# First quartic of the late images: a transpose on TensorE replaced by a block transpose on VectorE and four DMAs

## The chip, the cores and the metric

The kernel runs on one core of a Trainium2 chip. The metric is the device time of one execution in microseconds (us). Several executions of the kernel before gave 2962.28, 2969.88 and 2977.81 us, median 2969.88.

Names in the profile: PE is TensorE (PEld its weight loads), DVE is VectorE, ACT is ScalarE, POOL is GpSimd, SP is SyncE, which here only issues DMAs. SPq and ACTq are the DMA issues on those two engines.

## The reference, cut to what matters

```python
# x: 32 images, 32 channels, 128 x 128, float32
def layer0(A):                       # per image and channel: five steps of Newton-Schulz
    Y = A / norm(A); Z = I
    for _ in range(5):
        T = 0.5 * (3 * I - Z @ Y)
        Y = Y @ T
        Z = T @ Z
    return Y * sqrt(norm(A))
x = x + layer0(groupnorm(x))
def layer1(x):                       # 2-D Fourier transform, 64 x 32 modes, a channel product, back
    s = real(fft2(x))
    top = einsum('bixy,ioxy->boxy', s[:, :, :32, :32], weights1)
    bot = einsum('bixy,ioxy->boxy', s[:, :, -32:, :32], weights2)
    return real(ifft2(top and bot in a zero array))
x = x + layer1(groupnorm(x))
```

So each of the 1024 matrices of 128 x 128 goes through a polynomial in itself, and each image then through a transform, a product over channels and a transform back. The kernel merges the five steps into two quartics in the matrix, with the updates of `y` and `m` between them, and a last product.

## The kernel before

**Tiles and lanes.** A tile is four channels of one image, [128, 4, 128] floats, 256 KB; an image has 8 tiles, all images 256. One tile's Newton iteration is a Python generator, `newton` (line 479), with a `yield` between its steps. Up to 9 such generators are "lanes". The main loop (line 1132) runs in rounds; in each round every lane takes one step. `rest` is two yields. Whatever a step issues goes to the engines in that order, and an outer layer (`InOrder`, line 73) keeps the order of the program on every engine. Line 88 is the helper through which every instruction is recorded, so the profile shows L88 almost everywhere and groups are told apart by tile names.

**Far and near.** Images 1 to 18 are "far" (`is_far`, line 357): their transposed matrices are made by a 32 x 32 block transpose on DVE (`turned`, line 421) and DMAs that move the blocks (`across`, four DMAs of 64 KB from tile to tile; `away` and `back`, by way of DRAM). A new far tile starts every 26/9 rounds. Image 0 and images 19 to 31 are "near": transposes are done by TensorE (`transposed`, line 351), 4 per block. A new near tile starts every 5 rounds (`NEAR`), at most 5 lanes of them at a time (`LESS`); a near tile takes rounds 0 to 23 of its lane. There are 104 tiles in images 19 to 31.

**A near tile, by rounds of its lane.** `near_quartic` (line 407): in round 0 TensorE forms `products(mb, m)` (4 matmuls), DVE adds to make `v`; in round 1 POOL makes `r = mb + eye`; in round 2 TensorE transposes `v` and DVE makes `w` from that and `r`; in round 4 TensorE forms `products(v, w)` and DVE makes `q`; two rounds later it returns. Then `y` (round 6), the new matrix `m` (round 8), its transpose `mb` (TensorE and ACT, round 10), the second `near_quartic` (rounds 12 to 18), a pair of products of 256 columns (round 18), `t` (20) and the last product with DVE's addition to `xt` (22).

**Around the lanes.** `staged` (line 375) normalizes the next tile while a tile starts: `m` from `xt` (the transposed input) and `mb` from `b`. In near tiles POOL makes the four channels of `m` and ACT those of `mb`; in far tiles ACT makes two of the four of `m` as well. `fetch` (line 366) issues the two loads two tiles ahead, on SP for far images, on ACT for near ones. `prep` (line 222) loads an image pair's statistics input `xs` on the ACT queue, three loads ahead, one step per round while the first memory pools live. `settle` (line 538) stores a finished tile to `mid` on SP, and POOL folds it. Spectra and channel products follow per group of images (`GROUPS`, 20, 7, 3 and 2 images); `inverse` (line 970) runs beside the late lanes in three of ten rounds: it loads `yt` (512 KB each) on SP, TensorE transforms back, ACT copies `d`, DVE adds, POOL subtracts and adds `d` into `yt` (`unfold`), and `store` (line 932) writes `out` on SP at the next step of `inverse`. Images 0 to 19 are transformed back at about 1850 to 2390 us of the profile, the seven after them at about 2550 to 2750 us.

**Memory.** `rooms` (line 308) gives for each kind of tile how many buffers rotate in the pool that lives to the end and in the pool that is given up when the group of 20 images is nearly done (from tile 158 on only the first number counts). PSUM is 8 banks that rotate. A write into a rotated buffer waits until the last reader is done. A DMA is issued by its engine in order: where it must wait for data or a buffer, everything behind it on that engine waits too.

Of the kernel before, what the change touches and what calls it, by code (L numbers as in the profile page):

```python
# [31 lines left out]
ALU = mybir.AluOpType  # L32
# [16 lines left out]
MS = 1 / QR  # L49
# [44 lines left out]
def conv_preact_kernel(  # L94
# [49 lines left out]
        od.append(dram.tile(shape, F32, name=f"od{i}", tag=f"od{i}"))  # L144
    where = [(i, b) for i, n in enumerate(GROUPS) for b in range(n)]

    stp = ctx.enter_context(tc.tile_pool(name="stp", bufs=4))
    up = ctx.enter_context(tc.tile_pool(name="up", bufs=1))
    sp = ctx.enter_context(tc.tile_pool(name="sp", bufs=1))
    small = ctx.enter_context(tc.tile_pool(name="small", bufs=1))  # L150
# [71 lines left out]
    def prep(bs, made):  # L222

        n = len(bs)
        nc_, ng = n * C, n * G
        first_b = bs[0]
        st = small.tile([P, ng, 6], F32, tag="a_st", name=f"a_st{first_b}", bufs=2)
        tiles = []
        parts = [(b, i) for b in bs for i in range(C // 4)]

        ahead = 3 if first_b else 8

        def load(k):
            b, i = parts[k]
            if first_b or i < 4:
                t = stp.tile([P, 2, 2 * P], F32, tag="xs", name=f"xs{b}_{i}")
            else:
                t = four("turn", True).rearrange("p (j c) x -> p j (c x)", j=2)
            src = xs_in[b, :, 2 * i : 2 * i + 2].rearrange("p g h c -> p g (h c)")
            kept(nc.scalar.dma_start(out=t, in_=src))  # L240
            tiles.append(t)

        for k in range(ahead):
            load(k)
        yield
        for k in range(len(parts)):
            for j in range(2):
                nc.vector.bn_stats(st[:, 2 * k + j, :], tiles[k][:, j, :])
            yield
            if k + ahead < len(parts):  # L250
                load(k + ahead)
        ms = small.tile([P, ng], F32, tag="a_ms", name=f"a_ms{first_b}")
        nm, d = yield from moments(st, ms, "a")
        yield from pause
        pq = bank()[:, 0, 0:nc_]
        nc.tensor.matmul(pq, avg_mean, d.rearrange("p g c -> p (g c)"), start=True, stop=True)
        if not first_b:
            warm(5)

        v = small.tile([P, nc_ + ng], F32, tag="a_v", name=f"a_v{first_b}")  # L260
        nc.vector.tensor_scalar_mul(v[:, 0:nc_], pq, -512 / (P * P))
        yield
        vg = small.tile([P, ng], F32, tag="a_vg", name=f"a_vg{first_b}")
        nc.vector.tensor_reduce(
            vg, v[:, 0:nc_].rearrange("p (g c) -> p g c", c=2), AX.X, ALU.add
        )
        nc.vector.tensor_scalar(v[:, nc_:], vg, 0.5, EPS, ALU.mult, ALU.add)
        yield
        s = small.tile([P, nc_ + ng], F32, tag="a_r_s", name=f"a_r_s{first_b}", bufs=2)
        yield from root(v, nc_ + ng, s)  # L270
        iv = small.tile([P, nc_ + ng], F32, tag="a_inv", name=f"a_inv{first_b}")
        nc.vector.reciprocal(iv, s)
        yield

        sc = small.tile([P, nc_], F32, tag="a_sc", name=f"a_sc{first_b}", bufs=2)
        nc.vector.tensor_scalar_mul(sc, iv[:, 0:nc_], MS / P)
        off = small.tile([P, ng, 2], F32, tag="a_off", name=f"a_off{first_b}", bufs=2)
        nc.vector.tensor_tensor(
            off,
            sc.rearrange("p (g c) -> p g c", c=2),  # L280
            nm[:, :, None].to_broadcast([P, ng, 2]),
            ALU.mult,
        )
        off = off.rearrange("p g c -> p (g c)")
        sn = small.tile([P, nc_], F32, tag="a_t_s", name=f"a_t_s{first_b}", bufs=3)
        for k, b in enumerate(bs):
            g, c = slice(k * G, k * G + G), slice(k * C, k * C + C)
            made[b] = (nm[:, g], sc[:, c], off[:, c], sn[:, c])
        yield
        nn = small.tile([P, ng, 2], F32, tag="a_d", name=f"a_n{first_b}")  # L290
        nc.vector.tensor_tensor(
            nn,
            s[:, 0:nc_].rearrange("p (g c) -> p g c", c=2),
            iv[:, nc_:, None].to_broadcast([P, ng, 2]),
            ALU.mult,
        )
        nn = nn.rearrange("p g c -> p (g c)")
        for far in sorted({is_far(b) for b in bs}):
            of = [k for k, b in enumerate(bs) if is_far(b) == far]
            c = slice(of[0] * C, of[-1] * C + C)  # L300
            f = EYE_Q * QS if far else EYE * QF
            nc.vector.tensor_scalar_mul(nn[:, c], nn[:, c], P * (1.5 / f) ** 2)
        yield
        yield from root(nn, nc_, sn)
        yield


    rooms = dict(b=(4, 6), xt=(10, 5), x=(3, 2), r=(4, 0), v=(3, 2), w=(3, 2), q=(4, 2))
    rooms.update(my=(4, 3), mb=(2, 4), t=(3, 2), y4=(2, 2), turn=(0, 4))
    turns = dict.fromkeys(rooms, 0)  # L310

    def four(tag, more):
# [44 lines left out]
    def is_far(b):  # L357
        return 0 < b < FIRST
# [5 lines left out]
    raw = {}  # L364

    def fetch(b, g):
        queue = nc.sync if is_far(b) else nc.scalar
        xt, t = four("xt", has_more(b, g)), four("b", has_more(b, g))
        kept(queue.dma_start(out=t, in_=x[b, :, 4 * g : 4 * g + 4, :]))
        kept(queue.dma_start(out=xt, in_=xt_in[b, :, 4 * g : 4 * g + 4, :]))  # L370
        raw[b, g] = xt, t
# [3 lines left out]
    def staged(b, g, nm, sc, off, sn):  # L375
# [9 lines left out]

        for j in range(4):
            c = 4 * g + j
            if j < 2 or not is_far(b):
                kept(
                    nc.gpsimd.tensor_scalar(  # L390
                        m[:, j, :],
                        xt[:, j, :],
                        nm[:, c // 2 : c // 2 + 1],
                        sc[:, c : c + 1],
                        ALU.add,
                        ALU.mult,
                    )
                )
            else:
                on_scalar(m[:, j, :], xt[:, j, :], off, sc, c)  # L400
            on_scalar(mb[:, j, :], mb[:, j, :], off, sc, c)
            yield
# [4 lines left out]
    def near_quartic(m, mb, more):  # L407


        v = plus(m, -QA * MS, products(mb, m), "v", more)  # L410
        yield
        r = four("r", more)
        nc.gpsimd.tensor_tensor(r, mb, eye, ALU.add)
        yield
        w = plus(transposed(v), 1.0, r, "w", more)
        yield from rest
# [19 lines left out]
        kept(nc.sync.dma_start(out=into, in_=src))  # L436
        return t

    def by_rows(t):
        return blocks(t).rearrange("p a c j -> p c a j")  # L440

    def across(t, more):

        w = four("w", more)
# [7 lines left out]
            )  # L452
        return w

    def far_quartic(m, mb, v, f, later, more):

        ps = products(m, mb)
        if later:
            held = away(turned(ps, more))
        else:  # L460
            w = across(turned(ps, more), more)
        if later:
            yield
        nc.vector.scalar_tensor_tensor(v, ps, 1 / (9 * MS), v, ALU.mult, ALU.add)
        if not later:
            yield
# [9 lines left out]

    rest = (None, None)

    def newton(g, sn, xt, m, mb, v, far, more):


        qf, et, eye_t = (QS, EYE_Q, eye_q) if far else (QF, EYE, eye)
        if far:
            q = yield from far_quartic(m, mb, v, 1.0, False, more)
        else:
            q = yield from near_quartic(m, mb, more)
        my = four("my", more)
# [23 lines left out]
        else:  # L511
# [2 lines left out]
            mb = taken(transposed(m), "mb", more)  # L514
            yield from rest
            q = yield from near_quartic(m, mb, more)
            both = [bank().rearrange("p (j k) x -> p j k x", k=2) for _ in range(2)]
            for j in range(4):
                nc.tensor.matmul(both[j // 2][:, j % 2], q[:, j], my[:, j], start=True, stop=True)
# [223 lines left out]
    def small_products(i):  # L743
# [37 lines left out]
            load_weights(kk)  # L781
        for k2 in range(len(xks)):
            load_spectra(k2)
        done = None
        for kk in range(KK):
            yield
# [78 lines left out]
    def weights():  # L865


        kinds = [("b", 2)] * 3 + [("x", 2), ("b", 4), ("x", 4), ("x", 10)]
        kinds += [("my", 11)] * 2 + [("r", 12)] * 3 + [("mb", 15)] * 2 + [("v", 15)] * 2
        kinds += [("w", 16)] * 2 + [("my", 16), ("r", 17), ("v", 18)] + [("q", 19)] * 3  # L870
        first = B * C // 4 - 10
        spare = []
        for half in range(4, 2 * KK):
# [56 lines left out]
    stores = []  # L930

    def store():
        while stores:
            b, o, y = stores.pop(0)
            kept((nc.scalar if tail else nc.sync).dma_start(out=out[b, :, o : o + 8, :], in_=y))

    sums = []
# [2 lines left out]
    def unfold():  # L940

        while sums:
            b, o, y, d = sums.pop(0)
            engine = nc.vector if tail and o % 16 else nc.gpsimd
            for half, op in enumerate((ALU.subtract, ALU.add)):
                yh = y[:, :, 64 * half : 64 * half + 64]
                engine.tensor_tensor(yh, yh, d, op)
            stores.append((b, o, y))

    placed = {}  # L950

# [180 lines left out]
    while todo or any(lanes) or posts or specs or prods or backs:  # L1132
# [3 lines left out]
        for i in range(LANES):  # L1136
# [1 line left out]
            step(loads)  # L1138
            far = todo and is_far(todo[0][0])
            under_way = [is_far(lane[0]) for lane in lanes if lane]  # L1140
            room = far or under_way.count(False) + 0.6 * under_way.count(True) < LESS
            if lanes[i] is None and todo and room and rounds >= due:
                due = max(due, rounds - 1) + (FAR if far else NEAR)
                while norms:
                    step(norms)
                b, g = todo.pop(0)
                xt = ready[0][0]
                lanes[i] = (b, g, xt, newton(g, made[b][3], *ready.pop(0), far, has_more(b, g)))
                if stages:
                    stage()  # L1150
                if not todo:
# [11 lines left out]
                step(specs)  # L1163
            if i == 3 or tail:
                step(posts)
            turn = rounds % 10 in (0, 3, 7)
            if i == 0 and not turn or tail:
                step(prods)
# [72 lines left out]
```

## Time and profile before

| what | value |
|---|---|
| median of the runs | 2969.88 us |
| the profiled execution's own time | 2972.83 us |
| its span, first to last instruction | 2971.0 us |
| around the span | 1.8 us |
| granted clock of TensorE, mean | 0.987 |
| busy PE, DVE, POOL, ACT | 2847.8, 2270.9, 1986.9, 1544.7 us |
| HBM read and written | 402.42 MB, 229.11 MB |
| DMA, mean | 227 GB/s |

The busy shares are shares of the span. A group's line gives the count, the busy time in all, the mean duration of one in ns, and the idle time of its engine just before, with what ended that idle time. Matmuls overlap: the mean duration of one is longer than the distance from one to the next. A float32 matmul of 128 columns is two instructions in the profile, a transpose is one, so a block of four matmuls shows as x8 and a block of four transposes as x4. The span falls into: image 0 and the start (to about 60 us), the far images (to about 1500 us), near images alone or with the wide channel products (to about 1850 us), near images beside the way back of 20 images (to about 2390 us), channel products and the way back of seven (to about 2750 us), and the end.

### The profile page before, as it was taken

To read this page: it belongs to the slowest core of one execution; us is meant where nothing else is said; L and a number is where in the kernel's file an instruction comes from. 1 tells how busy PE (TensorE), PEld (TensorE's weight loads), DVE (VectorE), ACT (ScalarE), POOL (GpSimd) and SP (SyncE) were. 2 spreads that over 40 slices of the span, in tenths; PEclk is the share of its full clock that TensorE was granted. 3 is DMA by queue.
4 is the path that set the end of the run, shared out by engine and by line. 5 is a ranking of instruction groups with operands and counts; after the bars stand their busy time and mean duration, and the time that the engine had idled before them with its cause. 6 is when DMAs were issued, how large, how long until landed. Compare 5 with 4: busy or idle time off the path is not lost.

```text
span 2971.0 us, 74313 instructions
## 1 busy us (share of the span) xinstructions
PE 2847.8 (96%) x27688; PEld 2666.9 (90%) x27688; DVE 2270.9 (76%) x4407; ACT 1544.7 (52%) x3899; POOL 1986.9 (67%) x2308
## 2 busy tenths in 40 slices
PE   7999999999999999999999999999999999999995
PEld 7899999998999999999999889888888999888983
DVE  7779788888788888888886645886787766777565
ACT  3555555555555555555544445555555544655552
POOL 4677777776767777777665534877778764678453
PEclk9999999999999999999999999999999999999997
DMA  5687878787787878787843566767767747766577
GB/s 174 185 250 244 242 242 251 240 257 231 233 252 217 275 228 263 236 253 239 270 145 98 164 209 210 269 217 271 269 228 268 273 127 222 218 223 225 180 221 260
DMA packets 553078, 674.22 MB, mean 227 GB/s; under 512 B 99344, under 2 KB 333840, under 8 KB 552720
## 3 DMA queue, kind: packets, MB, share of 16 engines
q1 hardware_dynamic: 480576, 536.53, 56.9%
q10 hardware_dynamic: 72144, 132.94, 14.3%
q8 instruction: 222, 3.64, 0.5%
q14 instruction: 136, 1.11, 0.1%
HBM read 402.42 MB, written 229.11 MB: 213 GB/s over the span
## 4 chain that ended last, share of the span: by engine, by line
PE 66%; POOL 11%; DMA 9%; issue 7%; DVE 5%; ACT 1%; SPq 1%; ACTq 0%; DVEq 0%; POOLq 0%
PE ps L88 66%; POOL yt L88 3%; POOL r L88 3%; POOL x L88 2%; DMA w<-turn 2%; POOL fold L88 2%; DMA yt<-mid 1%; DMA b<-in_x 1%; DMA xt<-in_xt 1%; SPq L88 1%; DVE turn L88 1%; DMA xs<-in_xs 1%; DVE yt L88 1%; DMA mid<-xt 1%; DMA out<-yt 1%
## 5 line engine op out<-in xcount | busy, mean ns | idle before, releaser
L88 ACT ACTIVATE my<-ps 128x512 f32<-128x512 f32 x512 | 305.3, 600 | 563.6 <-PE ps L88 443.7
L88 POOL TENSOR_TENSOR fold<-xt 128x256 f32<-128x256 f32 x512 | 363.5, 732 | 285.9 <-DVE xt L88 257.2
L88 ACT ACTIVATE b<-b,a_off,a_sc 128x128 f32<-128x128 f32 x1024 | 469.8, 493 | 97.1 <-issue 15.9
L88 PE MATMUL ps<-my,q 128*128 128x128 f32 (+1 forms) x2944 | 474.4, 309 | 5.7 <-ACT my L88 3.8
L88 PEld LDWEIGHTS ps<-my,q 128*128 128x128 f32 x2944 | 412.9, 192 | 33.0 <-ACT my L88 4.6
L88 POOL TENSOR_TENSOR v<-eye_v,b 128x512 f32<-128x512 f32 x144 | 183.6, 1275 | 382.9 <-ACT b L88 344.6
L88 POOL TENSOR_TENSOR yt<-yt,d 128x512 f32<-128x512 f32 x244 | 306.8, 1281 | 187.4 <-ACT d L88 155.3
L88 PE MATMUL ps<-w,v 128*128 128x128 f32 x2944 | 399.9, 279 | 13.0 <-DVE w L88 10.6
L88 PEld LDWEIGHTS ps<-w,v 128*128 128x128 f32 x2944 | 363.5, 194 | 22.3 <-issue 7.6
L88 DVE STREAM_TRANSPOSE turn<-ps 128x512 f32<-128x512 f32 x432 | 299.7, 702 | 62.2 <-PE ps L88 57.1
L88 ACT ACTIVATE t<-ps 128x256 f32<-128x256 f32 (+1 forms) x368 | 171.0, 467 | 333.3 <-PE ps L88 316.7
L88 POOL TENSOR_SCALAR x<-xt,a_nm,a_sc 128x128 f32<-128x128 f32 x736 | 321.2, 450 | 15.8 <-DVE a_sc L88 15.5
L88 ACT ACTIVATE y<-ps,a_t_s 128x128 f32<-128x128 f32 x1024 | 291.4, 371 | 45.2 <-PE ps L88 45.1
L88 PE MATMUL ps<-q,t 128*128 128x128 f32 x2048 | 273.8, 277 | 0.8 <-DVE v L88 0.8
L88 DVE SCALAR_TENSOR_TENSOR w<-ps,r 128x512 f32<-128x512 f32 x224 | 153.1, 684 | 139.3 <-POOL r L88 71.2
L88 PEld LDWEIGHTS ps<-q,t 128*128 128x128 f32 x2048 | 249.6, 192 | 3.3 <-issue 1.2
L88 DVE BATCH_NORM_STATS2 a_st<-xs 128x6 f32<-128x256 f32 x504 | 185.9, 410 | 64.9 <-DMA xs<-in_xs 64.6
L88 DVE SCALAR_TENSOR_TENSOR q<-ps,eye 128x512 f32<-128x512 f32 x224 | 153.3, 684 | 97.6 <-PE ps L88 94.8
L88 DVE TENSOR_TENSOR xt<-ps,xt 128x512 f32<-128x512 f32 x256 | 174.7, 683 | 40.7 <-PE ps L88 35.2
L88 POOL TENSOR_TENSOR r<-mb,eye 128x512 f32<-128x512 f32 x112 | 142.9, 1276 | 91.8 <-ACT mb L88 91.8
L88 DVE TENSOR_TENSOR yt<-ps,yt 128x512 f32<-128x512 f32 x256 | 163.3, 681 | 39.9 <-PE ps L88 34.4
L88 POOL TENSOR_TENSOR my<-eye_q,my 128x512 f32<-128x512 f32 x144 | 183.8, 1277 | 7.5 <-PE ps L88 7.5
(147 smaller groups left out, 6284.9 us busy)
## 6 DMA issues: line engine op xcount, KB each, us to landing
turn<-turn SPq DMA_DIRECT2D x288, 256.0 KB
mid<-xt SPq DMA_DIRECT2D x256, 256.0 KB
yt<-mid SPq DMA_DIRECT2D x128, 512.0 KB
xs<-in_xs ACTq DMA_DIRECT2D x252, 256.0 KB
out<-yt SPq DMA_DIRECT2D x115, 512.0 KB
b<-in_x SPq DMA_DIRECT2D x144, 256.0 KB
xt<-in_xt SPq DMA_DIRECT2D x144, 256.0 KB
w<-turn SPq DMA_DIRECT2D x576, 64.0 KB
```

The costliest lines, as they stand in the source:

```text
L88: return self.tc.keep_in_program_order(issue(*args, **kw))
```

## The change

In the tiles of images 19 to 31, the first quartic no longer has a transpose on TensorE. `late_quartic` (new) makes: in round 0, on POOL `v = eye_v - m`, on TensorE `products(mb, m)`, on DVE the block transpose of that product out of PSUM; in round 1, on DVE `v` plus the product out of PSUM, on SP four DMAs of 64 KB that move the blocks from tile to tile (`across`); in round 2, on POOL `mb = eye_q - mb` in place; in round 6 `products(v, w)` with `w` read by rows of blocks, and DVE's `q`; it returns in round 8 instead of 6, so the tile takes rounds 0 to 25. A sixth near lane is allowed once no far lane is under way. The second quartic of these tiles, and both of image 0, keep the transpose; `r` there is issued in the quartic's first round in front of the products, where it was a round later.

Besides: two of the four channels of `m` of these tiles are made by ACT instead of POOL; their two loads are issued on SP instead of ACT; `prep` loads five ahead instead of three into 6 buffers instead of 4; a store of `out` is issued two rounds or more after POOL's sums, with an attempt in every round; the small channel products start two rounds later after their loads are issued; `rooms` and the order in which freed buffers take the last weights are dealt anew.

```diff
-    stp = ctx.enter_context(tc.tile_pool(name="stp", bufs=4))
+    stp = ctx.enter_context(tc.tile_pool(name="stp", bufs=6))
...
-        ahead = 3 if first_b else 8
+        ahead = 5 if first_b else 8
...
-    rooms = dict(b=(4, 6), xt=(10, 5), x=(3, 2), r=(4, 0), v=(3, 2), w=(3, 2), q=(4, 2))
-    rooms.update(my=(4, 3), mb=(2, 4), t=(3, 2), y4=(2, 2), turn=(0, 4))
+    rooms = dict(b=(5, 5), xt=(10, 4), x=(3, 2), r=(3, 0), v=(3, 2), w=(3, 2), q=(3, 3))
+    rooms.update(my=(3, 4), mb=(2, 4), t=(2, 3), y4=(2, 2), turn=(2, 2))
...
     def fetch(b, g):
-        queue = nc.sync if is_far(b) else nc.scalar
+        queue = nc.sync if b else nc.scalar
...
-            if j < 2 or not is_far(b):
+            if j < 2 or not b:
...
     def near_quartic(m, mb, more):
-        v = plus(m, -QA * MS, products(mb, m), "v", more)
-        yield
         r = four("r", more)
         nc.gpsimd.tensor_tensor(r, mb, eye, ALU.add)
+        v = plus(m, -QA * MS, products(mb, m), "v", more)
+        yield
         yield
         w = plus(transposed(v), 1.0, r, "w", more)
...
+    def late_quartic(m, mb, more):
+
+        v = minus(eye_v, m, four("v", more))
+        ps = products(mb, m)
+        t = turned(ps, more)
+        yield
+        nc.vector.scalar_tensor_tensor(v, ps, 1 / (9 * MS), v, ALU.mult, ALU.add)
+        w = across(t, more)
+        yield
+        minus(eye_q, mb, mb)
+        yield from rest
+        yield from rest
+        q = plus(products(v, by_rows(w)), 9 / (39 * MS**2), mb, "q", more)
+        yield from rest
+        return q
...
+        elif late:
+            q = yield from late_quartic(m, mb, more)
...
         for k2 in range(len(xks)):
             load_spectra(k2)
+        yield from rest
...
     def store():
-        while stores:
-            b, o, y = stores.pop(0)
+        while stores and (tail or rounds - stores[0][3] >= 2):
+            b, o, y, _ = stores.pop(0)
...
-            stores.append((b, o, y))
+            stores.append((b, o, y, rounds))
...
-            room = far or under_way.count(False) + 0.6 * under_way.count(True) < LESS
+            less = LESS if any(under_way) else LESS + 1
+            room = far or under_way.count(False) + 0.6 * under_way.count(True) < less
...
+            if i == 0:
+                store()
```

More of the change, by code (lines that the diff above doesn't have):

```diff
@@ L407, in near_quartic @@
     def near_quartic(m, mb, more):
+        r = four("r", more)
+        nc.gpsimd.tensor_tensor(r, mb, eye, ALU.add)
         v = plus(m, -QA * MS, products(mb, m), "v", more)
         yield
-        r = four("r", more)
-        nc.gpsimd.tensor_tensor(r, mb, eye, ALU.add)
         yield
@@ L437, in back @@
         return t
-    def by_rows(t):
-        return blocks(t).rearrange("p a c j -> p c a j")
     def across(t, more):
@@ L453, in across, with by_rows @@
         return w
+    def by_rows(t):
+        return blocks(t).rearrange("p a c j -> p c a j")
+    def late_quartic(m, mb, more):
[12 more added lines that the diff above has]
+        return q
     def far_quartic(m, mb, v, f, later, more):
@@ L459, in far_quartic @@
             held = away(turned(ps, more))
+            yield
         else:
             w = across(turned(ps, more), more)
-        if later:
-            yield
         nc.vector.scalar_tensor_tensor(v, ps, 1 / (9 * MS), v, ALU.mult, ALU.add)
@@ L477, in conv_preact_kernel, with newton @@
     rest = (None, None)
-    def newton(g, sn, xt, m, mb, v, far, more):
-        qf, et, eye_t = (QS, EYE_Q, eye_q) if far else (QF, EYE, eye)
+    def newton(g, sn, xt, m, mb, v, far, late, more):
+        qf, et, eye_t = (QS, EYE_Q, eye_q) if far or late else (QF, EYE, eye)
         if far:
             q = yield from far_quartic(m, mb, v, 1.0, False, more)
+        elif late:
+            q = yield from late_quartic(m, mb, more)
         else:
@@ L516, in newton @@
             q = yield from near_quartic(m, mb, more)
+            qf, et, eye_t = QF, EYE, eye
             both = [bank().rearrange("p (j k) x -> p j k x", k=2) for _ in range(2)]
@@ L865, in weights @@
     def weights():
-        kinds = [("b", 2)] * 3 + [("x", 2), ("b", 4), ("x", 4), ("x", 10)]
-        kinds += [("my", 11)] * 2 + [("r", 12)] * 3 + [("mb", 15)] * 2 + [("v", 15)] * 2
-        kinds += [("w", 16)] * 2 + [("my", 16), ("r", 17), ("v", 18)] + [("q", 19)] * 3
+        kinds = [("b", 3)] * 3 + [("x", 3), ("b", 6), ("x", 6), ("b", 10), ("x", 12)]
+        kinds += [("my", 13)] + [("r", 14)] * 2 + [("mb", 17)] * 2 + [("v", 17)] * 2
+        kinds += [("w", 18)] * 2 + [("my", 18), ("r", 19), ("v", 20), ("y4", 21)] + [("q", 21)] * 2 + [("q", 23)]
         first = B * C // 4 - 10
@@ L1147, in conv_preact_kernel @@
                 xt = ready[0][0]
-                lanes[i] = (b, g, xt, newton(g, made[b][3], *ready.pop(0), far, has_more(b, g)))
+                lanes[i] = (b, g, xt, newton(g, made[b][3], *ready.pop(0), far, b >= FIRST, has_more(b, g)))
                 if stages:
```

## The prediction

> **What bounds the kernel now.** I read the busy shares first, then the busy time by stage, then the chain, then the groups and waits of the stage that the change touches.
>
> Busy times of the whole span and the chain's shares by engine:
>
> ```profile
> span 2971.0 us, 74313 instructions
> ...
> PE 2847.8 (96%) x27688; PEld 2666.9 (90%) x27688; DVE 2270.9 (76%) x4407; ACT 1544.7 (52%) x3899; POOL 1986.9 (67%) x2308
> ...
> PE 66%; POOL 11%; DMA 9%; issue 7%; DVE 5%; ACT 1%; SPq 1%; ACTq 0%; DVEq 0%; POOLq 0%
> ```
>
> Busy times by stage (stretch, length, PE, PEld, DVE, ACT, POOL, clock, DMA share, GB/s): far, near alone, beside the way back of 20, beside the way back of seven:
>
> ```profile
> 300.00:1400.00 1100.00, 1073.33 (x9724) 1038.10 (x9723) 924.40 (x1821) 597.12 (x1524) 803.23 (x893) 1.00 0.80 244
> 1500.00:1650.00 150.00, 150.00 (x1310) 143.27 (x1310) 106.92 (x213) 70.34 (x179) 80.99 (x111) 1.00 0.37 117
> 1850.00:2400.00 550.00, 529.41 (x4688) 477.86 (x4687) 423.64 (x801) 288.70 (x758) 427.86 (x491) 0.99 0.73 249
> 2550.00:2750.00 200.00, 194.53 (x1703) 175.88 (x1702) 150.48 (x261) 114.73 (x281) 157.46 (x181) 0.98 0.65 218
> ```
>
> PE is full in every stage of the late images (96 to 100%; 97% and 100% in the two stretches with channel products between these), and only beside the way back is a second engine near it: POOL with 428 of 550 us. The chain says the same: it runs on PE except from 1850 to 2400 us, where most of its pieces are POOL's `yt`, `x` and `r`. So PE's work counts in full where POOL is light, and in part beside the way back.
>
> Groups of the whole span (count, busy us, mean ns, idle before):
>
> ```profile
> L88 PE MATMUL ps<-ident,v 128*128 128x128 f32 x896 | 137.9, 277 | 4.5 <-DVE xt L88 2.3 <-DVE v L88 2.2
> L88 POOL TENSOR_SCALAR x<-xt,a_nm,a_sc 128x128 f32<-128x128 f32 x736 | 321.2, 450 | 15.8 <-DVE a_sc L88 15.5
> L88 POOL TENSOR_TENSOR v<-eye_v,b 128x512 f32<-128x512 f32 x144 | 183.6, 1275 | 382.9 <-ACT b L88 344.6 <-PE ps L88 35.8 <-ACT b_r L88 2.5
> L88 DVE STREAM_TRANSPOSE turn<-ps 128x512 f32<-128x512 f32 x432 | 299.7, 702 | 62.2 <-PE ps L88 57.1 <-DMA w<-turn 1.1 <-DMA mb<-turn 0.2
> L88 DVE SCALAR_TENSOR_TENSOR w<-ps,r 128x512 f32<-128x512 f32 x224 | 153.1, 684 | 139.3 <-POOL r L88 71.2 <-PE ps L88 57.8 <-POOL x L88 8.5
> L88 ACT ACTIVATE x<-xt,a_off,a_sc 128x128 f32<-128x128 f32 x288 | 143.6, 499 | 9.5 <-DVE xt L88 2.5 <-DMA mb<-turn 2.4 <-DVE v L88 2.3
> ```
>
> PE in order of time, beside the way back (start, length, what); the distance between starts is what a block costs a full PE:
>
> ```profile
> 2011.15 1.06 PE L88 MATMUL ps<-w,v 128*128 128x128 f32 x8
> 2012.04 0.60 PE L88 MATMUL ps<-ident,v 128*128 128x128 f32 x4
> 2012.48 1.06 PE L88 MATMUL ps<-y,t 128*128 128x128 f32 x8
> ```
>
> Four matmuls take 0.89 us, four transposes 0.44 us. Waits in the far stage (300 to 1400 us), then three in 1600 to 2700 us, then the issue times of `across` and the like in the far stage (min/median/max ns):
>
> ```profile
> PE ps L88 <- DMA w<-turn: 15.4, 10, 5.2
> ...
> DVE a_st L88 <- DMA xs<-in_xs: 46.4, 21, 5.3
> ```
>
> ```profile
> DVE w L88 <- POOL r L88: 67.8, 33, 5.6
> ...
> ACT b L88 <- DMA mid<-xt: 14.0, 8, 3.2
> ACT b L88 <- POOL r L88: 13.1, 7, 7.7
> ...
> SPq L88 <- POOL yt L88: 201.4, 57, 6.3
> ```
>
> ```profile
> L88 SPq DMA_DIRECT2D w<-turn x558: 382/594/3805, 299.8 to 1399.5; - x186
> ```
>
> **The change part by part.** *Transposes.* 104 tiles lose 4 each, 416. By starts, 104 x 0.44 = 45.8 us of PE. Above: the group's busy share, 137.9/896 = 154 ns each, 64.0 us; below: nothing, where PE does not set the pace. I take the starts, since PE is full. `w` read by rows costs PE nothing new: the far stage reads it so, in the same group of 279 ns.
>
> The Trainium skill's "TensorE: Matmul & The Clock Gate", Part 4: PE-mode transpose, gives about 275 ns for one transpose inside a kernel; the row's 277 ns agrees as a length. By that figure the saving would be an estimated 114 us, which the distances between starts rule out.
>
> Where it counts: the way back lies beside 41 tiles in 1850 to 2400 us (41 `r<-mb,eye` there) and 15 in 2550 to 2750 us (60 of ACT's `y` copies, four a tile); 48 tiles lie elsewhere. Those 48 give 48 x 0.44 = -21.1 us. The 56 give between -24.6 us (PE paces) and what POOL adds: +1275 ns for `v`, +1275 for `mb`, -1275 for the first `r`, -2 x 450 for `x`, +375 ns a tile, 56 x 0.375 = +21 us (POOL paces). PE is idle 20.6 of 550 us there, POOL 122, so PE is nearer: I take 60% of PE's end, -14.8 us.
>
> *DVE.* A turn of 702 ns and two sums for three sums of 684: +18 ns a tile, 2 us, hidden by DVE's 24 to 30% of idle time; 0, at most +2. The product's PSUM bank is held one round longer, behind which PE may wait for DVE; for DVE's `v` PE waits 2.1 us and its weight loads 5.8 us in 1600 to 2700 us, so 0 to +8 us if that doubles, and I take 0, as the far tiles' later quartic holds a bank likewise.
>
> *ACT.* Two more `x` of 499 ns a tile, two DMA issues of 0.33 and 0.37 us less: +0.3 us a tile. ACT is half idle: 0; without that cover 31 us. The issues also leave with their waits: ACT stood behind late DMA slots and buffers (14.0 and 13.1 us above), which goes to SP. The loads are issued two tiles, 27 us, ahead, so SP may hold them back for long: 0; if not, `x` and `b` come late for POOL and ACT, at most what `b<-in_x` holds in the chain beside the way back, pieces of 6.5, 2.8 and 6.6 us.
>
> *SP and the DMAs.* SP gains 4 x 594 ns and two loads a tile, some 3.2 us of each 13.4 us (550/41); it is free for that. `across` stands on SP behind stores of `out` that wait for POOL (201.4 us of such waits; two rounds late they are mostly ready), stores of `mid` that wait for DVE, and the loads of `yt`. Its data are used five rounds after its issue, 13.4 us here; far tiles use it four rounds after, of 1100/122 x 9/26 = 3.1 us, 12.5 us. PE's wait for it there: 15.4 us over 122 tiles, 0.126 us a tile. Taken over: 104 x 0.126 = +13.1 us. Ends: 0, and in the worst case the rival below. More DMA work: 256 KB a tile over 249 GB/s x 13.4 us = 3.3 MB, 8%; the share of 0.73 becomes 0.79, as in the far stage (0.80).
>
> The skill speaks against this part: "DMA: Bandwidth & Descriptors", Rules for kernel authors, wants many small transfers made into one, with mostly overhead under 64 KB, and puts a DMA's fixed cost at about 2 us. As an estimate that is 416 x 2 = 832 us one after another, or 208 us if four overlap; the far stage's 15.4 us for 487 of them shows that the cost lies beside other work there, and no run here shows it beside the way back yet.
>
> *r in front.* The second `w` of a tile gets two rounds of POOL lead instead of one. The first quartic's `v` on POOL has one round before DVE needs it, as `r` had. So half of 67.8 us of DVE's waits go; on PE, waits for DVE's `w` were 6.2 us, and 5.8 us on PEld. I take -4 us; ends 0 and -12 (and +59 if POOL, at `r` earlier, waits as long for ACT's `mb` again as the 58.9 us it does now; that is idle POOL time, so it counts only if POOL paces).
>
> *xs five ahead.* DVE's 46.4 us of waits can go; the chain carries 15.2 us of them (pieces of 5.9, 5.1 and 4.2 us). I take half, -8 us; ends 0 and -46. The far stage loses one `xt` and one `r` buffer: a fetch came 11 to 20 us after its buffer 14 tiles back was free, so 0.
>
> *Late stores, later small products.* SP's waits shrink, and engines feel them only through loads of `yt` behind them, for which DVE waits 5.2 us in all: 0, within -5 and +5. PE's 4.9 us of waits for `plain<-xs` can go with the two rounds; that is inside the same ends. The new order of freed buffers for the last weights: PE shows no wait for such a load, 0.
>
> *The end.* The last tile takes two rounds more, 2 x 2.7 = +5 us; at the end less lies beside it.
>
> Sum: -21.1 - 14.8 + 13.1 - 4 - 8 + 5 = -29.8 us, 2943.0 for the profiled execution's 2972.83, which lies 3.0 us over the median. Against the median: 2940 us.
>
> **The rivals.** *POOL takes over beside the way back* (no change). For: the chain there, POOL 78% busy. Against: PE 96%. The 56 tiles give between 0 and +21 us instead of -14.8: sums of -15 to +6, 2955 to 2976 us.
>
> *`w` lands late* (slower). Place: PE's `products(v, w)` of the first quartic, round 6, behind which every lane's matmuls queue. For: SP's order, one ring with pairs of 512 KB, bursts of DMA beside the way back. Against: 0.126 us a tile in the far stage. It turns the forecast over when the wait exceeds (29.8 + 13.1)/104 = 0.41 us a tile; at 0.7 us, near one wait of 5.2 us (the longest seen) in seven tiles, -42.9 + 73 = +30, 3000 us.
>
> *More than the forecast.* All 56 tiles pay (-24.6), no waits for `w` (0), ACT freed of 27.1 us of blocked issues, half of it on the path (-14): -21.1 - 24.6 - 4 - 8 + 5 - 14 = -67, 2903 us.
>
> **How the numbers follow.** Forecast (2915 to 2955) 0.45; POOL 0.2; late `w` 0.17; more 0.18. About 0.5%, 15 us, is what can be told from no change. Faster: 0.45 + 0.18 + 0.05 of POOL's case = 0.68; same 0.16; slower 0.16. The range of 2900 to 2985 leaves out some 0.07 below and 0.13 above; the forecast's own is 2915 to 2955.
>
> **What would show it.** Right: 480 `ps<-ident,v` instructions instead of 896; starts 0.89 us apart around the late `products(v, w)`; PE still 95% or more from 1500 to 1850 us, and that stretch shorter by its tiles x 0.44 us; PE's waits for `w<-turn` under 15 us after 1600 us; `DVE w <- POOL r` halved; DVE's waits for `xs` near nothing. Wrong: PE's busy share beside the way back falls under 93% with POOL over 85% (POOL), or `DMA w<-turn` heads PE's waits there (late `w`).

## The result and the profile after

The changed kernel takes 2985.27 us (median), the kernel before 2967.89 us beside it: a ratio of 1.0061, 95% interval 1.0050 to 1.0072, 18 us slower. Forecast were 2940 us, with a chance of 0.68 for faster. The profiled execution took 2983.83 us, its span is 2981.7 us; the two profiled executions, before and after, lie 11 us apart, not 18.

The head of the page after, busy times of the whole span:

```profile
span 2981.7 us, 74377 instructions
...
PE 2815.0 (94%) x27272; PEld 2630.2 (88%) x27272; DVE 2290.9 (77%) x4407; ACT 1612.5 (54%) x4107; POOL 2026.5 (68%) x2204
```

The work moved in the directions read from the diff: PE has 416 instructions and 33 us less, ACT 68 us more, POOL 40 us more; DVE has 20 us more, where 2 were forecast. Only the time did not follow PE.

Busy times by stage after (stretch, length, PE, PEld, DVE, ACT, POOL, clock, DMA share, GB/s):

```profile
300.00:1400.00 1100.00, 1074.80 (x9702) 1040.28 (x9701) 927.23 (x1818) 593.90 (x1518) 802.91 (x892) 0.99 0.79 243
1500.00:1650.00 150.00, 146.89 (x1269) 139.79 (x1268) 109.30 (x219) 78.62 (x204) 86.17 (x100) 1.00 0.51 151
1850.00:2400.00 550.00, 508.75 (x4471) 456.00 (x4471) 434.48 (x786) 312.09 (x828) 437.34 (x441) 0.99 0.83 270
2550.00:2750.00 200.00, 189.79 (x1679) 171.02 (x1679) 154.26 (x272) 128.38 (x315) 159.18 (x162) 1.00 0.79 247
```

Beside the way back (the third row) PE fell from 529 to 509 of 550 us: what it was relieved of became idle time. No engine is full there; DVE, POOL and the DMA engines stand at 79 to 83%.

Where the time is, from the ends of DVE's 256 additions to `xt`, one per tile (us; "wide" holds the channel products of 20 images, "back" is beside the way back of 20):

| kernel | 152 to 164, near alone | 164 to 184, wide | 184 to 216, back | 216 to 256 | last tile to end |
|---|---|---|---|---|---|
| before | 127.3 | 283.6 | 424.2 | 507.9 | 65.5 |
| changed | 125.5 | 298.6 | 426.8 | 500.6 | 68.8 |

The far stage is the same (the 152nd addition ends at 1562.6 and 1561.4 us). Near alone 1.8 us are won, in the last 40 tiles 7.3 us, 15.0 us are lost beside the wide products, 2.6 beside the way back and 3.3 at the end. Each figure is from one execution: in five kernels of the experiments whose far stage is the same work, the 152nd addition ends anywhere from 1559.2 to 1575.4 us. So differences of a few us between stages are not clear of chance, here and below; the 15.0 us are the one that stands out.

Groups after (transposes on PE, the new `v` on POOL, the block transposes on DVE, POOL's share of `m`):

```profile
L88 PE MATMUL ps<-ident,v 128*128 128x128 f32 x480 | 73.0, 275 | 1.6 <-DVE v L88 1.6
L88 POOL TENSOR_TENSOR v<-eye_v,x 128x512 f32<-128x512 f32 x104 | 132.8, 1277 | 24.6 <-issue 22.6 <-DMA w<-turn 0.8 <-DMA diag<-xs 0.7
L88 DVE STREAM_TRANSPOSE turn<-ps 128x512 f32<-128x512 f32 x536 | 374.0, 704 | 166.6 <-PE ps L88 151.9 <-DMA w<-turn 4.6 <-DMA diag<-in_wk 2.8
L88 POOL TENSOR_SCALAR x<-xt,a_nm,a_sc 128x128 f32<-128x128 f32 x528 | 232.4, 451 | 16.2 <-DVE a_sc L88 15.3 <-PE ps L88 0.8
```

Counts and durations are those of the prediction. PE's waits from 1562 to 2750 us are not; the largest after are these (total us, times, longest):

```profile
PE ps L88 <- POOL fold L88: 17.4, 10, 2.7
PE ps L88 <- DMA plain<-xs: 10.5, 5, 4.2
PE ps L88 <- DVE q L88: 8.9, 9, 1.6
```

The late `w` is not among PE's waits there: PE does not stand behind its DMAs. It stands behind POOL's folds (1.8 us before) and behind operands of the wide products (`plain`, 4.9 us before).

### The profile page after: what moved, and what is told of

It is laid out like the page before. It is cut to its first block, busy times and chain, and to the rows that moved or that the text cites. A ratio compares the mean times of both kernels' runs of the same rounds, so it can differ in the third digit from the quotient of the medians.

```text
span 2981.7 us, 74377 instructions
## 1 busy us (share of the span) xinstructions
PE 2815.0 (94%) x27272; PEld 2630.2 (88%) x27272; DVE 2290.9 (77%) x4407; ACT 1612.5 (54%) x4107; POOL 2026.5 (68%) x2204
## 5 line engine op out<-in xcount | busy, mean ns | idle before, releaser
L88 ACT ACTIVATE b<-b,a_off,a_sc 128x128 f32<-128x128 f32 x1024 | 491.8, 500 | 43.5 <-DMA xs<-in_xs 22.9
L88 DVE STREAM_TRANSPOSE turn<-ps 128x512 f32<-128x512 f32 x536 | 374.0, 704 | 166.6 <-PE ps L88 151.9
L88 ACT ACTIVATE x<-xt,a_off,a_sc 128x128 f32<-128x128 f32 x496 | 250.5, 505 | 14.5 <-DMA xs<-in_xs 3.7
L88 POOL TENSOR_SCALAR x<-xt,a_nm,a_sc 128x128 f32<-128x128 f32 x528 | 232.4, 451 | 16.2 <-DVE a_sc L88 15.3
L88 DVE BATCH_NORM_STATS2 b_st<-xt 128x6 f32<-128x256 f32 x512 | 186.5, 404 | 0.0
L88 POOL TENSOR_TENSOR r<-eye_p,mb 128x512 f32<-128x512 f32 x144 | 183.4, 1274 | 0.9 <-DMA mb<-turn 0.9
```

The lines of the kernel that those rows point to most:

```text
L88: return self.tc.keep_in_program_order(issue(*args, **kw))
```

## The experiments

Ratios are to the kernel before in the same session; in us they are taken of 2968. The first theory, "POOL held", was that `r` in front makes POOL stand behind ACT's `mb`.

**The late quartic, and the side edits, apart.** Three runs undo parts of the change or do one alone. The first, in the changed kernel, has `r` a round behind the products again:

```diff
-        r = four("r", more)
-        nc.gpsimd.tensor_tensor(r, mb, eye, ALU.add)
         v = plus(m, -QA * MS, products(mb, m), "v", more)
         yield
+        r = four("r", more)
+        nc.gpsimd.tensor_tensor(r, mb, eye, ALU.add)
         yield
```

> The changed kernel with r issued a round behind the products again, as before. Theory 'POOL held': r in front makes POOL stand behind ACT's mb (142.1 us of such waits from 1600 to 2750 us, 58.9 us in 1600 to 2700 us before), so folds and v come late and PE waits for folds (17.4 us). It then expects those waits back near 60 us, PE's waits for folds under 5 us, and 15 to 30 us less time: 2955 to 2970. Theory 'SP and the ring' (the four DMAs and the loads now on SP delay what follows): no change within 5 us, 2980 to 2990.

1.0076 (1.0050 to 1.0102), no better than the changed kernel. The waits of POOL's `r` for `mb` fell from 149.2 to 55.8 us (1562 to 2750 us), the time did not fall; POOL waited longer elsewhere instead, for ACT's `d` 156.0 us (118.6). "POOL held" falls.

The second has the late quartic, its buffers and the sixth lane alone; against the changed kernel, in part:

```diff
+        queue = nc.sync if is_far(b) else nc.scalar
...
+            if j < 2 or not is_far(b):
...
+        while stores:
...
+        ahead = 3 if first_b else 8
```

> The late quartic, its buffers and the sixth lane alone; r, the loads' queue, the two channels of m, the stores, the xs depth and the small products as before. 'POOL held' expects nearly the whole forecast gain, 2925 to 2955, though POOL has 900 ns a tile more here than in the changed kernel (56 x 0.9 = 50 us of POOL beside the way back, idle time now). 'SP and the ring' expects 2975 or more, since the four DMAs are still on SP.

1.0235 (1.0208 to 1.0262), +70 us. The expectation had seen its 50 us more of POOL as idle time; this is the first sign that they are not.

The third has the side edits alone (loads on SP, two channels of `m` on ACT, `r` in front, later stores and small products), on the kernel before; three lines of it:

```diff
+        queue = nc.sync if b else nc.scalar
...
+            if j < 2 or not b:
...
+        while stores and (tail or rounds - stores[0][3] >= 2):
```

> The kernel before with the side edits alone: r in front, loads of the late images on SP, two channels of m on ACT, late stores, later small products; near quartics, buffers and xs depth as before. 'POOL held' expects a loss against the kernel before, 2975 to 2995, with POOL's waits for ACT's mb over 100 us. 'SP and the ring' expects 2960 to 2975.

0.9968 (0.9949 to 0.9987), 10 us faster. So the loss comes with the quartic (with its buffers and lane), 70 us by itself and 28 us on top of the side edits, and the side edits hide most of it.

**The price of what PE lost, in the changed kernel.**

```diff
         t = turned(ps, more)
         yield
+        transposed(m)
         nc.vector.scalar_tensor_tensor(v, ps, 1 / (9 * MS), v, ALU.mult, ALU.add)
```

> The changed kernel with four transposes of m per late tile added back on TensorE into a PSUM bank that nobody reads: the price of the removed work by itself. If PE paces the late stages, +46 us (104 x 0.44): 3025 to 3035. If PE's idle time takes it up, because the pace is set by waits elsewhere, under +15 us: 2985 to 3000.

1.0099 (1.0074 to 1.0123): putting 46 us of PE back costs 11 us (the intervals of the two kernels just clear each other). PE's idle time takes up the rest: its waits from 1562 to 2750 us fell from 72.1 to 51.6 us.

**Taking one suspect at a time from the changed kernel.** The first two leave a part of the quartic out, so they compute other numbers and serve only for the time. No moves (DVE's block transpose goes straight into `w`, and the blocks stay where they are):

```diff
-        t = turned(ps, more)
+        w = four("w", more)
+        nc.vector.transpose(blocks(w), ps.rearrange("p c (i b) -> p b c i", b=4))
         yield
         nc.vector.scalar_tensor_tensor(v, ps, 1 / (9 * MS), v, ALU.mult, ALU.add)
-        w = across(t, more)
```

> The changed kernel without the four DMAs of each late tile: DVE's turn writes w directly and the product reads it in place, so the moving of blocks between tiles is left out and the late tiles' numbers are not the reference's. Everything else is as in the changed kernel. Theory 'moves' (416 DMAs in SP's order and on its ring delay yt, mid, weights and w): 30 to 60 us less, 2920 to 2955. Theory 'POOL' (two more POOL operations of 1275 ns a tile make folds, yt and v late): no change, 2975 to 2990. Theory 'bank and v' (the product's bank is held a round longer, and DVE has one round to get v from POOL): no change, 2975 to 2990.

No subtraction on POOL:

```diff
         yield
-        minus(eye_q, mb, mb)
         yield from rest
```

> The changed kernel without POOL's subtraction eye_q - mb of each late tile (104 x 1275 ns = 133 us of POOL), which leaves that term out of the quartic, so its numbers are not the reference's. 'POOL' expects 20 to 40 us less, 2945 to 2965. 'Moves' and 'bank and v' expect 2975 to 2990.

The moves on ACT's queue:

```diff
-        w = across(t, more)
+        w = across(t, more, nc.scalar)
```

> The changed kernel with the late tiles' four DMAs issued by ACT instead of SP (104 x 4 x about 0.6 us = 250 us of issues on ACT, which is idle for 46%). 'Moves', if it is SP's order: 10 to 40 us less, 2945 to 2975. If it is the ring or the engines' shared DMA capacity, or 'POOL' or 'bank and v': no less than 2975, and up to 3010 as ACT now stands behind DMA slots.

`v` a tile ahead, the bank released in the same round:

```diff
+        v = minus(eye_v, mb if is_far(b) else m, four("v", has_more(b, g))) if b else None
...
-        v = minus(eye_v, m, four("v", more))
         ps = products(mb, m)
         t = turned(ps, more)
-        yield
         nc.vector.scalar_tensor_tensor(v, ps, 1 / (9 * MS), v, ALU.mult, ALU.add)
+        yield
```

> The changed kernel with v = eye_v - m made by POOL while the tile is normalized, a tile ahead, and DVE's sum out of the product's bank issued right behind its turn, in the same round (five v buffers at the end instead of three, one xt and one turn fewer). The bank is held a round less and DVE never waits for v. 'Bank and v' expects 15 to 40 us less, 2945 to 2970. 'Moves' and 'POOL' expect 2975 to 2990.

Without the moves 0.9971 (0.9958 to 0.9984), 27 us less; without the subtraction 0.9981 (0.9964 to 0.9998), 24 us less; moves on ACT 1.0202 (1.0177 to 1.0227), 42 us more; `v` ahead 1.0037 (1.0013 to 1.0062), 7 us less, but its interval meets the changed kernel's, so a gain is not shown. No theory has it alone: moves and POOL's subtraction cost about the same. Without the moves the 20 tiles beside the wide products take 282.9 us, as before (298.6 changed); without the subtraction the 32 beside the way back take 416.8 us (426.8). So each seems to cost mostly in a stage of its own, as far as one execution tells. The moves on ACT show what stands behind a DMA issue there; of ACT's waits from 1562 to 2750 us:

```profile
ACT mb L88 <- DMA w<-turn: 62.4, 16, 8.3
```

**More of the same, and both at once.** In turn: both suspects out; POOL making all of `m` again; the loads on ACT again; the first transform two rounds later.

```diff
-        w = across(t, more)
...
-        minus(eye_q, mb, mb)
```

> The changed kernel without the four DMAs and without POOL's subtraction of each late tile: the moving of blocks and one term are left out, so its numbers are not the reference's. POOL and DMA work per late tile then equal those of the side edits alone; what differs is 416 transposes less on TensorE, the turn on DVE, two rounds more per tile and a sixth lane. Theory 'PE paces once moves and POOL are out of the way': 46 us under the side edits alone (2958), 2905 to 2920. Theory 'late stages are paced by several engines' queues in turn, PE among them': 10 to 25 us under it, 2930 to 2950. Theory 'PE does not pace there at all': 2950 to 2960.

```diff
-            if j < 2 or not b:
+            if j < 2 or not is_far(b):
```

> The changed kernel with all four channels of m of the late tiles on POOL again (900 ns of POOL more a tile, 94 us; 1 us of ACT less). If POOL's work prices at what its subtraction did (24 us for 133 us): +17 us, 2995 to 3005. If POOL is not what counts: 2975 to 2988.

```diff
-        queue = nc.sync if b else nc.scalar
+        queue = nc.sync if is_far(b) else nc.scalar
```

> The changed kernel with the late tiles' loads on ACT again. If ACT stands behind DMA slots and buffers when it issues (as with the four moves on ACT, +44 us): +10 to +35 us, 2993 to 3018. If the loads only crowd SP: 2970 to 2985.

```diff
     def forward(b, q, u):
         yield
+        yield from rest
         fs = [folds.pop((b, 2 * q + i)) for i in range(2)]
```

> The changed kernel with the first transform of a finished half image two rounds later, so that PE no longer stands behind POOL's fold (17.4 us of PE's waits). If such waits are what POOL's extra work costs: 10 to 20 us less, 2962 to 2975. If they only stand in for other waits: 2978 to 2988.

Both out: 0.9923 (0.9902 to 0.9944), 13 us under the side edits alone, with the same POOL and DMA work and 46 us less on PE. That is the nearest to what taking the transposes away is worth: in the range of the expectation's second theory (several queues in turn), with intervals that barely clear each other, and with the buffers, the depth of `xs`, the sixth lane and two rounds a tile not equal. Against the changed kernel it is 41 us less, where the two suspects one by one gave 27 and 24. `m` on POOL: 1.0165 (1.0135 to 1.0196), +31 us for 94 us of POOL. Loads on ACT: 1.0152 (1.0119 to 1.0185), +27 us. Transform later: 1.0006 (0.9982 to 1.0030), -16 us; PE's waits for folds are gone there (17.4 us to none), so a schedule can take them away.

**Prices in the kernel before.** The prediction had set its prices there, so each kind of work was added to it alone, in round 1 of the late tiles' first quartic, with nobody reading the outcome. The transposes:

```diff
         r = four("r", more)
         nc.gpsimd.tensor_tensor(r, mb, eye, ALU.add)
+        if late:
+            transposed(m)
```

And in the next two kernels, in the place of the last line, POOL's subtraction and the moves:

```diff
+            minus(eye_q, mb, four("r", more))
```

```diff
+            across(m, more)
```

> The kernel before with four more transposes on TensorE per late tile (104 x 0.44 = 46 us), into a bank that nobody reads: the price of PE's work where the prediction took it. The prediction's step 'PE sets the pace in the late stages' expects +36 to +46 us, 3002 to 3012. 'Several queues in turn' expects about what the changed kernel showed, +10 to +20 us, 2975 to 2986.

> The kernel before with one more POOL subtraction per late tile (104 x 1275 ns = 133 us of POOL) into a buffer of its own that nobody reads. The prediction's step 'POOL's work is covered except beside the way back, and there PE is nearer' expects 0 to +20 us, 2966 to 2986. 'Several queues in turn' expects +20 to +50 us, 2986 to 3016.

> The kernel before with the four DMAs of 64 KB per late tile added in round 1 (they move m's blocks into a buffer that nobody reads; the loads stay on ACT, the stores early). Nobody waits for their data, so what shows is SP's order, DMA slots, ring and engines alone. The prediction took 0 for these. 'Moves delay the other DMAs' expects +20 to +40 us, 2986 to 3006; if it is only the wait for their data that counts, 2963 to 2975.

And the moves once more with a quarter of the bytes, 32 of the 128 columns of each block:

```diff
-            across(m, more)
+            across(m, more, P // 4)
```

> The kernel before with four DMAs per late tile as in the run that added moves by themselves (+1.36%, 40 us), but of a quarter of the bytes: as many DMAs, descriptors and slots, 128 bytes each instead of 512. If it is the number of DMAs in SP's order and in the slots (each DMA here waits for the one eight issues before it): +30 to +40 us, 2995 to 3008. If it is the bytes on the DMA engines: under +15 us, 2966 to 2982.

| added to the kernel before | work | ratio (95%) | us | 164 to 184 | 184 to 216 | 216 to 256 |
|---|---|---|---|---|---|---|
| nothing | | | | 283.6 | 424.2 | 507.9 |
| 416 transposes | 46 us of PE | 1.0095 (1.0078 to 1.0113) | +28 | 287.7 | 427.6 | 516.3 |
| 104 subtractions | 133 us of POOL | 1.0163 (1.0133 to 1.0192) | +48 | 287.1 | 455.0 | 514.8 |
| 416 moves | 27 MB | 1.0136 (1.0116 to 1.0156) | +40 | 294.6 | 435.8 | 519.0 |
| 416 small moves | 7 MB | 1.0113 (1.0094 to 1.0132) | +34 | 295.4 | 434.5 | 519.2 |

The ratios are of medians, the stages of one execution each. In these executions the stages from the 152nd tile on add up to 17.4, 39.7, 30.7 and 29.8 us more than before, in the table's order; the far stage, where nothing was added, differs by -3.4 to +12.8 us, the most in the run with PE's work. So the price of PE may be less than the 28 us of the medians.

Beside the way back (184 to 216) 40.8 us of POOL (32 x 1.275) cost 30.8 us: POOL sets the pace there, at a busy share that its own added work only raised from 428 to 448 of 550 us. 14.1 us of PE (32 x 0.44) cost 3.4 us there, which is not clear of chance, but far from POOL's. The stage with POOL's work added:

```profile
1850.00:2400.00 550.00, 512.75 (x4470) 460.00 (x4469) 419.60 (x758) 276.56 (x722) 448.27 (x497) 0.97 0.72 242
```

The moves cost 40 us though nobody waits for their data, and 34 us with a quarter of the bytes. The two intervals overlap, so a part that goes with the bytes is not shown; most of the price comes with their number. How it reaches PE is seen in the waits of the run with full moves, SP first, then ACT, then PE, 1562 to 2750 us; the rows of the kernel before follow in the same order:

```profile
SPq L88 <- DMA yt<-mid: 86.9, 58, 4.8
SPq L88 <- DMA b<-in_x: 35.1, 17, 6.2
...
ACT b L88 <- DMA yt<-mid: 23.3, 10, 4.9
...
ACT b L88 <- DMA w<-x: 15.4, 7, 8.6
...
PE ps L88 <- ACT my L88: 12.1, 7, 3.2
PE ps L88 <- ACT mb L88: 11.6, 5, 5.4
```

```profile
SPq L88 <- DMA yt<-mid: 45.3, 28, 3.6
...
SPq L88 <- DMA b<-in_x: 10.3, 6, 3.2
...
ACT b L88 <- DMA mid<-xt: 14.0, 8, 3.2
...
ACT b L88 <- DMA yt<-mid: 6.8, 3, 3.1
...
PE ps L88 <- ACT my L88: 3.5, 1, 3.5
PE ps L88 <- ACT mb L88: 3.1, 3, 2.0
```

SP and ACT hold a DMA back until an earlier, unrelated one has landed (`b`'s normalization on ACT comes right behind the loads that ACT issues). All rows of this kind together: SP's waits for DMAs grow from 143.3 to 256.7 us, ACT's from 31.8 to 112.6 us, PE's waits of all kinds from 31.6 to 55.2 us. ACT issues none of the moves, so the order on SP alone cannot be the reason. The trace shows what ties the two: the DMAs of SP and ACT share eight landing semaphores, about half of all issues wait themselves on the very semaphore that their own DMA will raise, and 45 of ACT's 46 waits for DMAs stand right behind an issue of its own. With more DMAs each of the eight comes round sooner. ACT's `my` and `mb` come later, and PE waits for them. With a quarter of the bytes the rows are nearly the same:

```profile
SPq L88 <- DMA yt<-mid: 86.4, 57, 4.8
...
PE ps L88 <- ACT my L88: 12.0, 7, 3.1
...
PE ps L88 <- ACT mb L88: 10.2, 5, 3.5
```

Each added piece of work also takes one buffer more per tile from a ring that rotates (a PSUM bank, an `r`, a `w`). For the moves this is not seen as a cost: none of the waits of DVE's `w` is for a DMA `w<-x`. In the changed kernel, where SP issues the loads, the moves show on SP as well: its waits for DMAs are 57.9 us without them and 167.7 us with them, PE's waits 49.8 and 72.1 us.

The Trainium skill, "DMA: Bandwidth & Descriptors", Rules for kernel authors, says that transfers under 64 KB are mostly overhead and that many small ones should be made one. The runs agree as far as they go: with a quarter of the bytes, 34 of the 40 us stay. The page's fixed cost of about 2 us for one DMA, given for the path by way of GpSimd, is no price of this kind: 40 us for 416 are 0.1 us of the kernel's time each. How much of the price is the order on SP and how much the limit on DMAs under way was not told apart.

**Versions that might beat both.** The later transform, with the side edits alone and no late quartic, and with `v` a tile ahead in the changed kernel:

```diff
     def forward(b, q, u):
         yield
+        yield from rest
```

> The side edits alone (r in front, loads on SP, two channels of m on ACT, late stores, later small products) with the first transform two rounds later as well. PE shows no waits for folds over 2 us there, so little is to be had: 2950 to 2960.

> The changed kernel with v a tile ahead (-7 us by itself) and the first transform two rounds later (-16 us by itself). If the two add up: 2958 to 2966, still over the side edits alone with the later transform (2952). If both remove the same waits: 2966 to 2976.

The first: 0.9949 (0.9929 to 0.9968), 15 us faster than the kernel before, the fastest that computes everything; its interval overlaps that of the side edits alone, so the later transform is not shown to add to them. The second, the changed kernel with `v` ahead and the later transform: 0.9994 (0.9975 to 1.0014), the same as the kernel before. The two gains (7 and 16 us) add up to 20 of 23 us. So the late quartic was brought to even; a gain from it is not shown, and the first version beats it by 13 us.

## Why the prediction was wrong

The step that failed first is "PE is full in every stage", from which the price of the transposes was taken: 35.9 us of gain were forecast, and taking them away was worth about 13. With it failed two terms: the DMAs, put at 0 apart from the wait for their data, which cost 27 us in the changed kernel and 40 in the kernel before, and POOL's added work beside the way back, which was taken to matter less than PE's and came out as time to three quarters.

*Transposes: count and duration right, price too high.* The instructions fell from 896 to 480, and the block of four is gone from between its neighbours. PE in order of time, after (start, length, what):

```profile
2031.26 1.06 PE L88 MATMUL ps<-x,q 128*128 128x128 f32 x8
2032.16 1.06 PE L88 MATMUL ps<-w,v 128*128 128x128 f32 x8
2033.05 1.06 PE L88 MATMUL ps<-y,t 128*128 128x128 f32 x8
```

Forecast were 35.9 us of gain (21.1 + 14.8). In the kernel before, 46 us of PE added cost 28 us, or 17 by its late stages; with moves and subtraction left out, their absence gave 13 us; in the changed kernel putting them back cost 11 us. 96% busy meant that PE nearly always had something under way, not that its work set the pace.

*"PE is idle 20.6 of 550 us there, POOL 122, so PE is nearer": wrong.* Most of POOL's idle time beside the way back is a wait in its order, for ACT's `d` (95.4 of the 122 us) and DVE's `xt` (16.2 us), and new work mostly does not fit into it: three quarters of POOL's came out as time, and those two waits still stood at 75.7 and 17.3 us with it. Over all late stages before (1562 to 2750 us) the waits are:

```profile
POOL fold L88 <- DVE xt L88: 177.8, 48, 13.3
POOL yt L88 <- ACT d L88: 127.4, 38, 7.6
```

The chain had said so, POOL beside the way back, and the busy shares were believed instead. POOL's net +39 us (104 x 0.375), at 0.36 us per us (48/133), is an estimated +14 us over the late stages, where the sum had POOL in only one bound. The signs that the prediction named for this rival came by half: PE beside the way back fell under 93%, to 92.5%, but POOL stood at 79.5% and not over 85%.

*The moves: the wrong question.* The +13.1 us were for PE's wait for the data. That wait did not come, and the rival "`w` lands late" is refuted, though its sign was right. The reason is not the one given, a longer slack: the 15.4 us and the 122 tiles belong to 200 to 1400 us and not to 300 to 1400, so a far round is 3.4 us and four of them 13.6, as long as the late tiles' 13.4. Why the wait of the far stage did not carry over stays open. The cost was 40 us in the kernel before and 27 us in the changed one, from what the DMAs do to other DMAs. "It is free for that" looked at SP's issue time and not at what it waits for. This is the largest missing term.

*The sum with the measured prices.* For the quartic alone, with one POOL operation more a tile (+2 - 1): -28 + 48 + 40 = +60 us, and +75 with the 13 us of PE's work taken away in place of the 28 of work added; measured +70. The two sums lie on either side of it, so what is left is within what the prices are known to. The bank held a round longer, `v`'s one round (`v` ahead: -7 us, not clear of its interval), a sixth lane, two rounds more and the buffers dealt anew are in the +70 and were not priced by themselves.

*ACT and SP: loads and `m` at 0, wrong in the good direction.* With the quartic in place, the loads on SP are worth 27 us and two channels of `m` off POOL 31 us. Without the quartic all the side edits together give 10 us. That they pay where POOL and the DMAs are strained fits this, but was not tested by itself.

*DVE:* its idle time in the late rows is 23 to 29%, not 24 to 30; nothing rests on that. *r in front, -4 us:* taking it back cost 4 us, not distinguishable from 0; DVE's waits of `w` for `r`, 67.8 us before, are gone, and the time did not show it. *xs five ahead, -8 us:* DVE's waits in the far stage went from 46.4 to 9.0 us. In the twelve profiled kernels with five ahead the 152nd addition ends at 1560.6 us on average, in the eight with three at 1565.6 (most of these have other buffers too); with a spread of 1552.4 to 1575.4 us, some 5 of the 8 us are likely but not shown. *The end, +5 us:* +3.3 us; but the side edits alone, without two rounds more, have 70.3 us there (65.5 before), so the reason given is not shown.

*POOL as rival (2955 to 2976):* the right mechanism for half of it; with the moves' price its sum would have ended above the kernel before.

## What to carry to other kernels

An engine at 96% whose neighbours wait on it in order need not be the pace: add its work, in a buffer that nobody reads, to the kernel as it is, and do so for each engine that a change loads, before trading one for another. Here a microsecond of added work was worth 0.6 on the busiest engine and 0.36 on the one with a third of its time idle (0.38 and 0.30 by the late stages of one execution), and the change moved 46 us off the first for 39 us and 416 DMAs more elsewhere. Price a DMA by what is queued behind it, not only by who waits for its data.

## What the runs showed that was not expected

Four DMAs of 16 KB a tile cost the kernel 34 us in 104 tiles, those of 64 KB 40 us. The same DMAs issued by ACT instead of SP cost 42 us more, with ACT 46% idle. Beside the way back POOL, with a fifth of its time idle, took new work at three quarters of its length; PE, with 4% idle, took it at about a quarter, as far as one execution tells.
